# A graph attention network on one core: edges matched with sliding spans of 128 nodes, no running maximum, node work inside the edge loops

## The chip, the core and the metric

The kernel runs on one core of a Trainium2 chip. The engines are called here as the profile calls them: PE (TensorE; matmuls, and PEld its weight loads), DVE (VectorE), ACT (ScalarE), POOL (GpSimd, which also issues the indirect DMAs), SP (SyncE, which issues DMAs). The metric is the device time of one execution in microseconds (us), the median of several runs. A profile is one execution taken by the hardware profiler.

## What is computed

A graph has 6250 nodes and 100,000 edges (src, dst), sorted by dst, some 16 edges to a node, and an edge from each node to itself. Nodes have 768 numbers, all in float32. The reference, cut to what matters:

```python
def gat_conv(x, src, dst, W, a_src, a_dst, bias, heads):
    n = x.shape[0]
    h = (x @ W).reshape(n, heads, -1)
    alpha_s = (h * a_src[None]).sum(-1)
    alpha_d = (h * a_dst[None]).sum(-1)
    e = leaky_relu(alpha_s[src] + alpha_d[dst], 0.2)
    m = segment_max(e, dst, num_segments=n)
    e = exp(e - m[dst])
    denom = segment_sum(e, dst, num_segments=n)
    alpha = e / (denom[dst] + 1e-16)
    out = segment_sum(h[src] * alpha[:, :, None], dst, num_segments=n)
    return out.reshape(n, -1) + bias

# src, dst below: the edges and the loops
h = maximum(layernorm(x), 0)
h = relu(gat_conv(h, src, dst, W1, a_src1, a_dst1, b1, 4))   # 768 -> 4 heads of 64
h = relu(gat_conv(h, src, dst, W2, a_src2, a_dst2, b2, 1))   # 256 -> 1 head of 256
return x + relu(h @ Wm1 + bm1) @ Wm2 + bm2                   # 256 -> 256 -> 768
```

## The kernel before

Nodes lie in 49 tiles of 128 (the partitions). Edges lie in 98 chunks of 1024, each of 8 tiles of 128. Five stages follow one another:

1. **Nodes, first layer** (L187 to L211): for each node tile a layernorm, six transposes on PE (`tp`, L175) with evictions on DVE (`xT`, L176), six matmuls `h_ps` (L210); `keep_nodes` works out both scores with two products and a reduction on DVE (`pr`, `state`), puts features and source score as a row into a table in DRAM (`table<-row`) and the node's own edge into the accumulator `acc`.
2. **Edges, first layer** (`edges_in`, 98 chunks). `gather`: POOL issues 8 indirect DMAs, each of 128 rows of the table (`G`, L219); the source scores are transposed, stored to DRAM (`s_d`), and in `along` read back along the free dimension into all partitions (`S`, 512 KB per head) beside the chunk's destinations (`drow`, 512 KB). `greatest`: for the two node tiles that a chunk may reach, starting at a tile number loaded into a register, DVE makes the masks `mask` (nodes in the partitions), `pen` and `hot` (edges in the partitions), finds each node's greatest score (the fused add-and-maximum of L269, twice per head), and works out the new maximum `m` and the factor `fade` by which earlier sums shrink. `add`: matmuls `e_ps` with `mask` as the weights (L300, two for each edge tile) bring each edge its end's maximum and score, ACT takes the exponential, `hw` is the weighted rows, matmuls `o_ps` (L327, two for each edge tile) with `hot` as the weights sum them by node, and DVE scales and adds (`kept`, `acc`, L332 and L334).
3. **Nodes, second layer**: `aggregated` divides, adds the bias on POOL (`ob`, L398), applies relu and transposes; then matmuls `h_ps` (L412) and `keep_nodes`.
4. **Edges, second layer**: as 2, with one head; `hw` is made on ACT.
5. **Dense layers** (L428 to L449): `aggregated`, matmuls `m_ps` (L436) and `y_ps` (L445), residual, store.

A table can be gathered from only when all its rows are written, so each edge stage starts after all of the node stage ahead of it. All instructions of one engine run in one order; that order is not the one of the source but is fixed at build time by the framework's scheduler. Chunks that reach more than two node tiles would go through a loop behind each edge stage (L370); it turns zero times with these data. Matmuls of float32 operands appear in the profile as two records each.

Of the kernel before, what the change touches and what calls it, by code (L numbers as in the profile page):

```python
# [15 lines left out]
ENG = mybir.EngineType  # L16

P = 128
N = 6250          # nodes
E = 100000        # edges, self loops apart  # L20
# [6 lines left out]

NT = -(-N // P)   # node tiles
NTP = NT + 1      # and an empty one, so that two tiles can always be taken at once
TPC = 8           # edge tiles in a chunk  # L30
CH = P * TPC      # edges in a chunk
NCH = -(-E // CH)
PAD_DST = 1 << 20  # the destination of padding edges: no node
# [3 lines left out]
def kernel(  # L37
# [7 lines left out]
    a_src1: bass.AP,  # L45
    a_dst1: bass.AP,
    b1: bass.AP,
    W2: bass.AP,
    a_src2: bass.AP,
    a_dst2: bass.AP,  # L50
# [16 lines left out]
    dram_as = pool("dram_as", 4, space=bass.MemoryType.DRAM)  # L67
    sm = pool("sm", 3)
# [7 lines left out]
    ident = const.tile([P, P], F32, name="ident")  # L76
    make_identity(nc, ident)
    pidx = const.tile([P, 2], F32, name="pidx")
    nc.gpsimd.iota(pidx, pattern=[[P, 2]], base=0, channel_multiplier=1,
                   allow_small_or_imprecise_dtypes=True)  # L80
    iota2 = const.tile([P, 2 * P], F32, name="iota2")
    nc.gpsimd.iota(iota2, pattern=[[1, 2 * P]], base=0, channel_multiplier=0,
                   allow_small_or_imprecise_dtypes=True)
    first = const.tile([P, NTP], F32, name="first")
    nc.gpsimd.iota(first, pattern=[[P, NTP]], base=0, channel_multiplier=0,
                   allow_small_or_imprecise_dtypes=True)
    eps_c = const.tile([P, 1], F32, name="eps_c")
    nc.vector.memset(eps_c, EPS)

    att = {}  # L90
    for layer, s, d, b in ((1, a_src1, a_dst1, b1), (2, a_src2, a_dst2, b2)):
        for kind, v in (("s", s), ("d", d), ("b", b)):
            t = const.tile([P, HID], F32, name=f"att{layer}{kind}")
            nc.scalar.dma_start(t, bcast(v, HID))
            att[layer, kind] = t

# [1 line left out]
    src_i = const.tile([P, NCH * TPC], I32, name="src_i")  # L98
    nc.scalar.dma_start(src_i, src_cols)
    dst_f = const.tile([P, NCH * TPC], F32, name="dst_f")  # L100
    once = ctx.enter_context(ExitStack())
    ones = once.enter_context(tc.tile_pool(name="once", bufs=1))
    dst_i = ones.tile([P, NCH * TPC], I32, name="dst_i")
    nc.scalar.dma_start(dst_i, dst_cols)
    nc.vector.tensor_copy(dst_f, dst_i)

    dri = ones.tile([NCH, CH], I32, name="dri")
    nc.scalar.dma_start(dri, dst_rows)
    drf = ones.tile([NCH, CH], F32, name="drf")
    nc.vector.tensor_copy(drf, dri)  # L110
    dstf_d = dram.tile([NCH, CH], F32, name="dstf_d")
    nc.scalar.dma_start(dstf_d, drf)
    ends = const.tile([P, 2], F32, name="ends")
    nc.vector.tensor_reduce(ends[:NCH, 0:1], drf, AX.X, ALU.min)
    real = ones.tile([NCH, CH], F32, name="real")
    nc.vector.tensor_scalar(real, drf, float(N - 1), None, ALU.min)
    nc.vector.tensor_reduce(ends[:NCH, 1:2], real, AX.X, ALU.max)
    ends_i = const.tile([P, 2], I32, name="ends_i")
    nc.vector.tensor_copy(ends_i[:NCH], ends[:NCH])
    ends_t = const.tile([P, 2], I32, name="ends_t")  # L120
    nc.vector.tensor_scalar(ends_t[:NCH], ends_i[:NCH], 7, None, ALU.arith_shift_right)
    lohi_d = dram.tile([NCH, 2], I32, name="lohi_d")
    nc.scalar.dma_start(lohi_d, ends_t[:NCH])
    lohi = const.tile([1, NCH, 2], I32, name="lohi")
    nc.scalar.dma_start(lohi, bass.AP(tensor=lohi_d.tensor, offset=lohi_d.offset,
                                      ap=[[0, 1], [2, NCH], [1, 2]]))
    span = const.tile([1, NCH], F32, name="span")
    nc.vector.tensor_sub(span, lohi[:, :, 1], lohi[:, :, 0])
    wide = const.tile([1, 1], F32, name="wide")
    nc.vector.tensor_reduce(wide, span, AX.X, ALU.max)  # L130
    more = const.tile([1, 1], I32, name="more")
    nc.vector.tensor_scalar(more, wide, 2.0, float(NCH), ALU.is_ge, ALU.mult)
    once.close()

# [1 line left out]
    acc = const.tile([P, NTP, 4, HID // 4 + 1], F32, name="acc")  # L136
    nc.gpsimd.memset(acc[:, NT], 0.0)
    accf = acc.rearrange("p n h c -> p n (h c)")
    RW = 4 * (HID // 4 + 1)
    state = {}  # L140
    table = {}
    for layer, H in ((1, 4), (2, 1)):
        state[layer] = const.tile([P, NTP, 2, H], F32, name=f"state{layer}")
        nc.gpsimd.memset(state[layer][:, NT], 0.0)
        table[layer] = dram.tile([NT * P, HID + H], F32, name=f"table{layer}")

    def acc_view(H, sl):
        C = HID // H
        return accf[:, sl, :H * (C + 1)].rearrange("p n (h c) -> p n h c", h=H)

    def keep_nodes(wk, layer, H, i, h_ps):
        """A tile of nodes' features: into the table, and each node's own edge."""
        C = HID // H
        st = state[layer]
        row = wk.tile([P, HID + H], F32, name="row", tag="row")
        nc.scalar.activation(row[:, :HID], h_ps, AF.Copy)
        hv = h_ps.rearrange("p (h c) -> p h c", h=H)
        pr = wk.tile([P, 2, HID], F32, name="pr", tag="pr")
        nc.vector.tensor_mul(pr[:, 0], h_ps, att[layer, "s"])
        nc.vector.tensor_mul(pr[:, 1], h_ps, att[layer, "d"])  # L160
        nc.vector.tensor_reduce(st[:, i], pr.rearrange("p k (h c) -> p k h c", h=H), AX.X, ALU.add)
        nc.vector.tensor_copy(row[:, HID:], st[:, i, 0])
        av = acc_view(H, slice(i, i + 1))[:, 0]
        nc.scalar.activation(av[:, :, :C], hv, AF.Copy)
        nc.vector.memset(av[:, :, C:], 1.0)
        nc.sync.dma_start(table[layer][i * P:(i + 1) * P], row)

    def transposed(wk, t, k, name):
        """[128, k * 128] -> [128, k, 128], with each block transposed."""
        o = wk.tile([P, k, P], F32, name=name, tag=name)  # L170
        for k0 in range(0, k, 4):
            n = min(4, k - k0)
            p = ps.tile([P, 4, P], F32, name="tp", tag="tp")
            for j in range(n):
                nc.tensor.transpose(p[:, j], t[:, (k0 + j) * P:(k0 + j + 1) * P], ident)  # L175
            nc.vector.tensor_copy(o[:, k0:k0 + n], p[:, :n])  # L176
        return o
# [65 lines left out]
    def greatest(pools, layer, H, dcol, drow, S, b):  # L243
# [17 lines left out]
        for t in range(TPC):  # L261
            nc.vector.tensor_scalar(hot[:, t], iota2, drel[:, t:t + 1], None, ALU.is_equal)  # L262
# [218 lines left out]
```

## Time and profile before

| | |
|---|---|
| runs, us | 4979.31 median, 4977.9 to 4987.44 (3 runs) |
| span of the profiled execution | 5039.1 us, the only time that the profile gives for it |
| busy in it | PE 71%, DVE 65%, POOL 35%, ACT 15% of the span |
| first gather of layer 1, of layer 2 | 294.4 us, 3041.7 us |
| moved by DMA | 648 MB, 129 GB/s in the mean |

The profiled execution's span is 1.2% above the median of the runs. A row of a group reads: line, engine, operation, output<-inputs, shapes, count | busy us, mean ns of one | idle time of the engine just before them, and what ended it. A row of the timeline reads: start, duration (us), engine, line, operation, names, count and in brackets the idle time before it.

### The profile page before, as it was taken

The numbers are of one execution on the slowest core, as the hardware profiler recorded it, in microseconds if no ns is written. First come the engines' busy times: TensorE is split into PE (matmuls) and PEld (weight loads), VectorE is DVE, ScalarE is ACT, GpSimd is POOL, SyncE is SP. The second block draws the span as 40 slices with busy tenths as digits, with TensorE's granted clock in tenths as the row PEclk, the third lists the DMA queues.
The fourth block names the chain that finished last, engine by engine and source line by source line (L and its number), as shares of the span: only waits on it lengthen the run. The fifth ranks groups of instructions, "written<-read, shape, count | busy, mean of one in ns | idle before, by whom it ended". The sixth has DMA issues, their size and how long they took to land. (4 is left out here: it accounts for less than half of the span.)

```text
span 5039.1 us, 49714 instructions
## 1 busy us (share of the span) xinstructions
PE 3571.8 (71%) x14798; PEld 3086.7 (61%) x14799; DVE 3269.3 (65%) x9030; ACT 731.7 (15%) x2257; POOL 1783.9 (35%) x1728
## 2 busy tenths in 40 slices
PE   5636666666666666666666665888888888888888
PEld 4535555555555555555555544777777777777766
DVE  6757777777777777777777684555555555556544
ACT  3310000000000000000000031222222222222222
POOL 0033333333333333323333125344444444343345
PEclk9966666666666666666666676777777777777789
DMA  3344444444444444444444113333333333333345
GB/s 116 101 145 143 147 139 139 141 142 147 147 136 139 143 144 148 140 134 143 143 147 142 67 47 121 118 119 120 122 118 120 116 120 116 119 118 117 101 140 178
DMA packets 219275, 648.07 MB, mean 129 GB/s; under 512 B 42915, under 2 KB 61428, under 8 KB 218998
## 3 DMA queue, kind: packets, MB, share of 16 engines
q1 hardware_dynamic: 113060, 330.58, 19.3%
q0 software_dynamic: 75264, 207.63, 14.8%
q10 hardware_dynamic: 30674, 106.61, 5.9%
q8 instruction: 119, 1.95, 0.2%
q14 instruction: 158, 1.29, 0.1%
HBM read 610.07 MB, written 34.58 MB: 128 GB/s over the span
## 5 line engine op out<-in xcount | busy, mean ns | idle before, releaser
L219 POOL DMA_INDIRECT G<-table,src_i x1568 | 1624.3, 1036 | 2893.6 <-ACT hw L321 732.1
L327 PE MATMUL o_ps<-hw,hot 128*128 128x260 f32 (+1 forms) x6272 | 1755.7, 448 | 520.1 <-DVE hw L318 270.4
L327 PEld LDWEIGHTS o_ps<-hw,hot 128*128 128x128 f32 x6272 | 1419.0, 230 | 796.2 <-issue 522.0
L300 PE MATMUL e_ps<-m,mask 128*128 128x8 f32 (+1 forms) x6272 | 1323.7, 350 | 170.6 <-DVE m L281 170.6
L300 PEld LDWEIGHTS e_ps<-m,mask 128*128 128x128 f32 x6272 | 1321.4, 325 | 175.9 <-issue 136.2
L269 DVE CUSTOM_DVE_ANT_0 junk<-pen,S 128x1024 f32<-128x1024 bf16 x980 | 1193.5, 1218 | 38.1 <-DMA S<-s_d 19.6
L334 DVE TENSOR_TENSOR acc<-kept,o_ps 128x520 f32 (+1 forms) x196 | 135.8, 693 | 869.9 <-remote 592.7
L225 PE MATMUL s_ps<-ident,s_in 128*32 128x128 f32 (+1 forms) x196 | 63.7, 325 | 594.4 <-ACT s_in L224 512.1
L262 DVE TENSOR_SCALAR hot<-iota,drel 128x256 f32<-128x256 f32 x1568 | 448.3, 357 | 0.1
L303 DVE TENSOR_TENSOR z<-G,e_ps 128x32 f32<-128x32 f32 (+1 forms) x196 | 34.6, 177 | 623.0 <-PE e_ps L300 599.6
L225 PEld LDWEIGHTS s_ps<-ident,s_in 128*32 128x32 f32 (+1 forms) x196 | 17.8, 91 | 673.5 <-ACT s_in L224 582.4
L316 ACT ACTIVATE hw<-G,wt 128x256 f32<-128x256 f32 x784 | 323.7, 496 | 1.6
L224 ACT ACTIVATE s_in<-G 128x32 f32<-128x32 f32 (+1 forms) x196 | 46.4, 236 | 1820.9 <-DMA G<-table,src_i 1776.6
L258 DVE TENSOR_SCALAR mask<-drow,nid 128x1024 f32<-128x1024 f32 x392 | 298.3, 761 | 5.7 <-DMA drow<-dstf_d 5.7
L259 DVE TENSOR_SCALAR pen<-drow,nid 128x1024 bf16<-128x1024 f32 x392 | 293.6, 749 | 0.0
L318 DVE TENSOR_TENSOR hw<-G,wt 128x2048 f32<-128x2048 f32 x98 | 224.1, 2287 | 0.4 <-ACT wt L312 0.3
L210 PE MATMUL h_ps<-w,xT 128*128 128x256 f32 x588 | 146.3, 401 | 79.2 <-DVE xT L176 67.7
L312 ACT ACTIVATE wt<-dn 128x32 f32<-128x32 f32 (+1 forms) x196 | 42.9, 219 | 1006.3 <-DVE dn L310 846.5
L210 PEld LDWEIGHTS h_ps<-w,xT 128*128 128x128 f32 x588 | 113.1, 199 | 104.6 <-ACT xn L206 48.3
L288 ACT ACTIVATE fade<-fall 128x8 f32<-128x8 f32 (+1 forms) x196 | 39.6, 202 | 707.6 <-DVE fall L286 707.6
L445 PE MATMUL y_ps<-wm,mT 128*128 128x384 f32 x392 | 139.8, 500 | 3.1 <-ACT mT L440 1.2
L332 DVE TENSOR_TENSOR kept<-acc,fade 128x520 f32<-128x520 f32 (+1 forms) x196 | 135.4, 691 | 0.1
(81 smaller groups left out, 1949.3 us busy)
## 6 DMA issues: line engine op xcount, KB each, us to landing
S<-s_d SPq DMA_DIRECT2D x490, 512.0 KB
drow<-dstf_d ACTq DMA_DIRECT2D x196, 512.0 KB
xt<-in_x SPq DMA_DIRECT2D x96, 384.0 KB
G<-table,src_i POOLq DMA_INDIRECT x1568
out<-y SPq DMA_DIRECT2D x48, 384.0 KB
table<-row SPq DMA_DIRECT2D x49, 130.0 KB
table<-row SPq DMA_DIRECT2D x49, 128.5 KB
s_d<-s_sb SPq DMA_DIRECT2D x98, 16.0 KB
```

The lines of the kernel that those rows point to most:

```text
L210: nc.tensor.matmul(h_ps, xT[:, k], w1[:, k], start=(k == 0), stop=(k == KI - 1))
L219: nc.gpsimd.indirect_dma_start(out=G[:, t], out_offset=None, in_=table[layer], in_offset=bass.IndirectOffsetOnAxis(ap=idx[:, t:t + 1], axi ...
L258: nc.vector.tensor_scalar(mask[:, w], drow, nid[:, w:w + 1], None, ALU.is_equal)
L259: nc.vector.tensor_scalar(pen[:, w], drow, nid[:, w:w + 1], -BIG, ALU.not_equal, ALU.mult)
L262: nc.vector.tensor_scalar(hot[:, t], iota2, drel[:, t:t + 1], None, ALU.is_equal)
L269: nc.vector.tensor_tensor_reduce(out=junk, in0=pen[:, w], in1=S[h], scale=1.0, scalar=-BIG, op0=ALU.add, op1=ALU.max, accum_out=top[:, w, ...
L300: nc.tensor.matmul(e_ps[:, t], mask[:, w, t * P:(t + 1) * P], m[:, w, 1:3], start=(w == 0), stop=(w == 1))
L316: nc.scalar.activation(hw[:, t, 0, :C], G[:, t, :HID], AF.Copy, scale=wt[:, t])
L318: nc.vector.tensor_mul(hw[:, :, :, :C], G[:, :, :HID].rearrange("p t (h c) -> p t h c", h=H), wt.unsqueeze(3).to_broadcast([P, TPC, H, C]))
L327: nc.tensor.matmul(o_ps[:, w, :H * (C + 1)], hot[:, t, w * P:(w + 1) * P], hw[:, t].rearrange("p h c -> p (h c)"), start=(t == 0), stop=(t ...
L334: nc.vector.tensor_add(accf[:, ds(b, 2), :H * (C + 1)], kept[:, :, :H * (C + 1)], o_ps[:, :, :H * (C + 1)])
L445: nc.tensor.matmul(y_ps[:, s, :half], mT[:, j], wm2[:, j, s * half:(s + 1) * half], start=(j == 0), stop=(j == KH - 1))
```

## The change

The kernel is rewritten; the table gains a column of ones for each head.

- **Spans.** Edges are shifted by 256 empty ones and taken in 196 groups of 512 (4 tiles), one for each 32 nodes. Group g is matched with the 128 nodes from 32g - 64 on, so each edge tile has one span of nodes, not two tiles of them. Two groups (8 edge tiles) are a step u; there are 98 steps. Of 784 edge tiles 782 are worked on.
- **No maximum.** The weight of an edge, over a factor common to all edges of its end, is max(exp(s), exp(0.2 s) rho) with s the source's score and rho = exp(-0.8 d) of the end's score d. `prepare` makes rho for all nodes before a layer's edges, splits it into three bfloat16 parts and lays it out by spans (`win`). An edge gets rho by one bfloat16 matmul for each edge tile (`e_ps`, weights `mask`). `S`, `s_d`, `pen`, `top`, `fade`, `kept` and the register loads are gone.
- **Sums.** Each group's `o_ps` is added to the running span `acc`, of which the 32 nodes that left are cleared by `keep`; 32 finished nodes at a time are copied to `sum` by ACT.
- **Node work in the loops.** When a node tile is finished its own edge, division, transposes and matmuls (stages 3 and 5 above) run as `steps`, one step in each turn of the edge loop. Scores come out of the node matmuls as extra columns (`with_scores`). Nothing but gathers is left on POOL in the edge loops.
- **General path.** At the end four flags (a score above 20 in either layer, an edge below or above its span) decide whether the old algorithm runs over everything (`general`).

Its core, new lines alone (`G` has 5 buffers, `rows` 2, `hot` 3, `mask` and `hw` 2, each tag in PSUM 2):

```diff
+        s, d = sd[layer][:, :, :H], sd[layer][:, :, H:]
+        rho = wk.tile([P, NT, H], F32, name="rho")
+        nc.scalar.activation(rho, d, AF.Exp, scale=SLOPE - 1.0)
...
+        e1 = wk.tile([P, NT, H], F32, name="e1")
+        nc.scalar.activation(e1, s, AF.Exp)
+        e2 = wk.tile([P, NT, H], F32, name="e2")
+        nc.scalar.activation(e2, s, AF.Exp, scale=SLOPE)
+        v = wk.tile([P, NT, H], F32, name="v")
+        nc.vector.tensor_mul(v, e2, rho)
+        own = wk.tile([P, NT, H], F32, name="own")
+        nc.vector.tensor_max(own, v, e1)
...
+            def gather(u):
+                G = gp.tile([P, 8, TW[layer]], F32, name="G")
+                for t in tiles(u):
+                    k = 8 * u + t
+                    nc.gpsimd.indirect_dma_start(
+                        out=G[:, t], out_offset=None, in_=table[layer],
+                        in_offset=bass.IndirectOffsetOnAxis(ap=src_i[:, k:k + 1], axis=0))
+                return G
...
+            def match(u):
+                if u % 2 == 0:
+                    drow[0] = rows.tile([P, 2, 8 * P], BF16, name="drow")
+                    n = min(2, NU - u)
+                    nc.sync.dma_start(
+                        drow[0][:, :n].rearrange("p u e -> p (u e)"),
+                        bcast(dmod_d, n * 8 * P, u * 8 * P))
+                T = tiles(u)
...
+                mask = eg.tile([P, 8 * P], BF16, name="mask")
+                nc.vector.tensor_tensor(mask[:, t0 * P:(t0 + n) * P],
+                                        drow[0][:, u % 2, t0 * P:(t0 + n) * P],
+                                        pidx_b.to_broadcast([P, n * P]), ALU.is_equal)
+                hot = eg.tile([P, 8, P], F32, name="hot", bufs=3)
+                nc.vector.tensor_tensor(
+                    hot[:, t0:t0 + n], iota.unsqueeze(1).to_broadcast([P, n, P]),
+                    dcol[:, 8 * u + t0:8 * u + t0 + n].unsqueeze(2).to_broadcast([P, n, P]),
+                    ALU.is_equal)
+                e_ps = ps.tile([P, 8, 3 * H], F32, name="e_ps", tag="tp")
+                for t in T:
+                    g = 2 * u + t // TPG
+                    nc.tensor.matmul(e_ps[:, t], mask[:, t * P:(t + 1) * P], win[:, g + 1],
+                                     start=True, stop=True)
+                return hot, e_ps
...
+                sc = G[:, T, RW[1]:] if layer == 1 else G[:, T, HID:HID + 1]
+                e1 = sm.tile([P, 8, H], F32, name="e1")
+                nc.scalar.activation(e1[:, T], sc, AF.Exp)
+                e2 = sm.tile([P, 8, H], F32, name="e2")
+                nc.scalar.activation(e2[:, T], sc, AF.Exp, scale=SLOPE)
+                rho = sm.tile([P, 8, H], F32, name="rho")
+                nc.vector.tensor_reduce(rho[:, T], e_ps[:, T].rearrange("p t (h k) -> p t h k", k=3),
+                                        AX.X, ALU.add)
+                v = sm.tile([P, 8, H], F32, name="v")
+                nc.vector.tensor_mul(v[:, T], e2[:, T], rho[:, T])
+                w = sm.tile([P, 8, H], F32, name="w")
+                nc.vector.tensor_max(w[:, T], v[:, T], e1[:, T])
+                if layer == 2:
+                    hw = eg.tile([P, 8, P], F32, name="hw")
+                    nc.vector.tensor_mul(hw[:, T], hot[:, T],
+                                         w[:, T].to_broadcast([P, n, P]))
+                else:
+                    hw = eg.tile([P, 8, H, C + 1], F32, name="hw")
+                    nc.vector.tensor_mul(
+                        hw[:, T], G[:, T, :RW[1]].rearrange("p t (h c) -> p t h c", h=H),
+                        w[:, T].unsqueeze(3).to_broadcast([P, n, H, C + 1]))
+                return hw
...
+                    T = [t for t in tiles(u) if t // TPG == half]
+                    o_ps = ps.tile([P, RW[layer]], F32, name="o_ps", tag="o")
+                    for t in T:
+                        if layer == 2:
+                            l, r = hw[:, t], G[:, t]
+                        else:
+                            l, r = hot[:, t], hw[:, t].rearrange("p h c -> p (h c)")
+                        nc.tensor.matmul(o_ps, l, r, start=(t == T[0]), stop=(t == T[-1]))
...
+                        nc.vector.tensor_copy(acc, o[half])
+                    else:
+                        nc.vector.scalar_tensor_tensor(acc, run[0], keep[:, (g + 1) % 4:(g + 1) % 4 + 1],
+                                                       o[half], ALU.mult, ALU.add)
...
+                        nc.scalar.activation(done[t][r], acc[r], AF.Copy)
...
+            for i in range(NU + 3):
+                a, b, c, d = i, i - 1, i - 2, i - 3
+                if a < NU:
+                    G[a] = gather(a)
+                if 0 <= d < NU:
+                    o = spread(d, G.pop(d), H_.pop(d)[0], W_.pop(d))
+                if 0 <= b < NU:
+                    H_[b] = match(b)
+                if 0 <= c < NU:
+                    W_[c] = weigh(c, G[c], *H_[c])
+                if 0 <= d < NU:
+                    gather_up(d, o)
+                advance()
...
+        def mean1(t, sum_, own):
+            C = HID // 4
+            mine = wk.tile([P, 4, C + 1], F32, name="mine")
+            nc.vector.tensor_mul(mine, heads_row(rows1.pop(t)),
+                                 own[:, t].unsqueeze(2).to_broadcast([P, 4, C + 1]))
+            all_ = wk.tile([P, 4, C + 1], F32, name="all_")
+            nc.vector.tensor_add(all_, mine, sum_.rearrange("p (h c) -> p h c", h=4))
+            rden = wk.tile([P, 4], F32, name="rden")
+            nc.vector.reciprocal(rden, all_[:, :, C])
+            o = wk.tile([P, HID], F32, name="o")
+            nc.vector.tensor_mul(o.rearrange("p (h c) -> p h c", h=4), all_[:, :, :C],
+                                 rden.unsqueeze(2).to_broadcast([P, 4, C]))
+            return o
...
+        layer_edges(1, 4, [mean1, lambda t, o, own: turned(wk, 1, o), features2], fetch1)
...
+        layer_edges(2, 1, [mean2, lambda t, o, own: turned(wk, 2, o), dense1, dense2], fetch2)
...
+    is_bad = nc.values_load(bad_i, min_val=0, max_val=1)
+    with tc.If(is_bad):
+        general(ctx, tc, locals())
```

**How the order of instructions changes.** First place: the edge loop of layer 1, in its steady course. On PE stood, chunk by chunk (s_ps is the transpose of the scores):

```order
L225 MATMUL s_ps<-ident,s_in 32x128
L300 MATMUL e_ps<-m,mask 128x8 x16
L327 MATMUL o_ps<-hw,hot 128x260 x16
L225 MATMUL s_ps<-ident,s_in 32x128
L300 MATMUL e_ps<-m,mask 128x8 x32
```

Now the same engine has, the pair of its first two rows eight times in each step:

```order
L305 LDWEIGHTS mask
L305 MATMUL e_ps<-win,mask 128x12
L348 MATMUL o_ps<-hw,hot 128x260 x8
L408 MATMUL tp<-ident,o 128x128 x2
L441 MATMUL h_ps<-w_2073,rT 128x258
```

For 8 edge tiles there are 8 matmuls with `hot` where there were 16, and 8 with `mask` where there were 16; a transpose pair and two `h_ps` stand in every second step. On DVE, same place, one of the two parts of a chunk was:

```order
L251 TENSOR_SCALAR nid<-pidx,base 128x2
L281 SCALAR_TENSOR_TENSOR m<-both 128x2x8
L318 TENSOR_TENSOR hw<-G,wt 128x32x64
L286 TENSOR_TENSOR fall<-m 128x8
L253 TENSOR_SCALAR drel<-dst_f,base 128x8
L258 TENSOR_SCALAR mask<-drow,nid 128x1024
L259 TENSOR_SCALAR pen<-drow,nid 128x1024
L258 TENSOR_SCALAR mask<-drow,nid 128x1024
L259 TENSOR_SCALAR pen<-drow,nid 128x1024
L269 ISA junk,top<-pen,S 128x1024
L269 ISA top 128x1
```

Now DVE has, over some more than one step (`acc` twice in a step, once for each half):

```order
L363 SCALAR_TENSOR_TENSOR acc<-acc,keep,o_ps 128x260
L298 TENSOR_TENSOR hot<-iota,dcol 128x1024
L430 TENSOR_TENSOR all__2602<-mine,sum 128x260
L320 TENSOR_REDUCE rho<-e_ps 128x32
L432 RECIPROCAL rden<-all__2602 128x4
L363 SCALAR_TENSOR_TENSOR acc<-acc,keep,o_ps 128x260
L434 TENSOR_TENSOR o<-all__2602,rden 128x256
L323 TENSOR_TENSOR v<-e_2642,rho 128x32
L294 TENSOR_TENSOR mask<-drow,pidx_b 128x1024
L325 TENSOR_TENSOR w<-v,e_2640 128x32
L363 SCALAR_TENSOR_TENSOR acc<-acc,keep,o_ps 128x260
L332 TENSOR_TENSOR hw<-G,w 128x2080
```

The eight rows of L269 for a chunk are gone, `mask` and `hot` are one instruction each, and `all_`, `rden` and `o` of the node work stand between them; here the second `acc` of a step stands ahead of the next step's `hw`.

Second place: the edge loop of layer 2 on PE. Before:

```order
L225 MATMUL s_ps<-ident,s_in 8x128
L300 MATMUL e_ps<-m,mask 128x2 x32
L327 MATMUL o_ps<-hw,hot 128x257 x16
L225 MATMUL s_ps<-ident,s_in 8x128
L327 MATMUL o_ps<-hw,hot 128x257 x16
```

Now, over two steps (with `m_ps` x4 between the next `e_ps`):

```order
L305 MATMUL e_ps<-win,mask 128x3
L498 MATMUL y_ps<-wm_8366,mT 128x384
L348 MATMUL o_ps<-G,hw 128x258 x8
L498 MATMUL y_ps<-wm_8366,mT 128x384 x3
L408 MATMUL tp<-ident,o 128x128 x2
L348 MATMUL o_ps<-G,hw 128x258 x8
```

The dense layers' matmuls, a stage of their own before, have moved between the edge matmuls.

More of the change, by code (lines that the diff above doesn't have):

```diff
@@ L131 @@
[L131 to L177, printed above, removed]
+    ones_c = const.tile([P, 1], F32, name="ones_c")
+    nc.vector.memset(ones_c, 1.0)
@@ new lines @@
+    TW = {1: RW[1] + 4, 2: RW[2]}
+    table, sd = {}, {}
+    for layer, H in heads.items():
+        table[layer] = dram.tile([NT * P, TW[layer]], F32, name=f"table{layer}")
+        sd[layer] = const.tile([P, NT, 2 * H], F32, name=f"sd{layer}")
+    bT = {}
+    for layer, b in ((1, b1), (2, b2)):
+        bT[layer] = const.tile([P, KH], F32, name=f"bT{layer}")
+        with nc.allow_non_contiguous_dma(reason="256 numbers"):
+            nc.scalar.dma_start(bT[layer], b.rearrange("(k p) -> p k", p=P))
@@ L206 @@
             nc.scalar.activation(xn, xt, AF.Relu, bias=shift, scale=rstd)
-            xT = transposed(wk, xn, KI, "xT")
-            h_ps = ps.tile([P, HID], F32, name="h_ps", tag="mm")
+            xT = wk.tile([P, KI, P], F32, name="xT")
+            for k0 in range(0, KI, 4):
+                n = min(4, KI - k0)
+                p = ps.tile([P, 4, P], F32, name="tp", tag="tp")
+                for j in range(n):
+                    nc.tensor.transpose(p[:, j], xn[:, (k0 + j) * P:(k0 + j + 1) * P], ident)
+                nc.vector.tensor_copy(xT[:, k0:k0 + n], p[:, :n])
@@ L209 @@
+            h_ps = ps.tile([P, HID + 8], F32, name="h_ps", tag="mm")
             for k in range(KI):
                 nc.tensor.matmul(h_ps, xT[:, k], w1[:, k], start=(k == 0), stop=(k == KI - 1))
[L211 to L230 removed]
```

717 lines of the change are left out of this document (466 added, 251 removed).

## The prediction

> **What bounds the kernel now.** I read the page's busy times first, then busy times by stage, the waits, the groups and short stretches of the timeline.
>
> ```profile
> span 5039.1 us, 49714 instructions
> PE 3571.8 (71%) x14798; PEld 3086.7 (61%) x14799; DVE 3269.3 (65%) x9030; ACT 731.7 (15%) x2257; POOL 1783.9 (35%) x1728
> ```
>
> No engine fills the span. By stage (columns: stretch, its length, busy us and count of PE, PEld, DVE, ACT, POOL, then granted PE clock, DMA share, GB/s):
>
> ```profile
> 0.00:294.40 294.40, 179.28 (x882) 148.74 (x883) 201.93 (x626) 98.63 (x198) 1.59 (x13) 0.97 0.31 99
> 294.40:2806.00 2511.60, 1561.38 (x6136) 1364.29 (x6136) 1821.51 (x4368) 118.42 (x480) 868.30 (x784) 0.66 0.44 144
> 2806.00:3041.70 235.70, 153.26 (x530) 112.10 (x529) 175.27 (x571) 55.31 (x158) 35.68 (x49) 0.70 0.13 43
> 3041.70:4835.00 1793.30, 1487.59 (x6383) 1331.17 (x6384) 975.34 (x3252) 414.84 (x1278) 759.77 (x789) 0.72 0.38 117
> 4835.00:5040.00 205.00, 190.27 (x871) 130.42 (x869) 95.28 (x214) 44.53 (x143) 118.51 (x93) 0.97 0.54 183
> ```
>
> Rows 2 and 4 are the edge stages, 85% of the span: 25.6 us a chunk in layer 1 (DVE 73% busy, PE 62%), 18.3 in layer 2 (PE 83%). POOL works a third to two fifths of both and stands the rest:
>
> ```profile
> ACT s_in L224 <- DMA G<-table,src_i: 1776.6, 192, 16.9
> ACT wt L312 <- DVE dn L310: 846.5, 102, 19.0
> POOL G L219 <- ACT hw L321: 732.1, 47, 17.2
> DVE z L303 <- PE e_ps L300: 599.6, 194, 7.7
> ```
>
> So gathers wait for a buffer that the arithmetic frees, and the arithmetic waits in turns between DVE and PE. This is what the change cuts, and the question is what comes next.
>
> **POOL's price.** The change leaves 782 gathers for each layer (784 before). First all gathers, then those of the first 41 us of layer 1, then what DVE did in those 41 us:
>
> ```profile
> L219 POOL DMA_INDIRECT G<-table,src_i x1568 | 1624.3, 1036 | 2893.6 <-ACT hw L321 732.1 <-DVE drel L253 544.5 <-DVE fall L286 525.6
> L219 POOL DMA_INDIRECT G<-table,src_i x32 | 31.5, 983 | 301.7 <-DMA table<-row 292.2 <-issue 9.4
> L269 DVE CUSTOM_DVE_ANT_0 junk<-pen,S 128x1024 f32<-128x1024 bf16 x9 | 11.0, 1225 | 22.2 <-issue 14.9 <-DMA S<-s_d 7.1
> L258 DVE TENSOR_SCALAR mask<-drow,nid 128x1024 f32<-128x1024 f32 x4 | 3.2, 804 | 5.7 <-DMA drow<-dstf_d 5.7
> ```
>
> 32 gathers without a wait for anything took 31.5 us and 9.4 of "issue" between them: (31.5 + 9.4) / 32 = 1.28 us each. The quickest and a slow one:
>
> ```profile
> 1009.22 0.74 DVE L258 TENSOR_SCALAR mask<-drow,nid 128x1024 f32<-128x1024 f32 x1
> 1009.36 1.42 POOL L219 DMA_INDIRECT G<-table,src_i  x1 [17.75 <-DVE fall L286]
> ...
> 1020.27 0.95 POOL L219 DMA_INDIRECT G<-table,src_i  x1 [0.30 <-issue]
> 1024.31 0.26 ACT L224 ACTIVATE s_in<-G 128x32 f32<-128x32 f32 x1 [14.90 <-DMA G<-table,src_i]
> ```
>
> The floor is 0.95 + 0.30 = 1.25 us with DVE still; beside `mask` (one input, 1024 in 0.74 us) a gather took 1.42; with the mean of all it is 1.036 + 0.30 = 1.34. A gather has landed 3.1 us after its end (1021.22 to 1024.31). Step u needs 8 gathers: 10.0, 10.2 or 10.7 us. I take 1.28, since the changed loop has no instruction like `mask` of L258 left, but many with two inputs like L269, which filled 11 of those 41 us. Ends: 1.25 and 1.34.
>
> The Trainium skill's page "SBUF — State Buffer", section "Who interferes with whom", speaks against this: a DVE instruction with two SBUF inputs shuts out a GpSimd instruction that reads SBUF, for its whole length, and nearly all of DVE's work here now is such. By the same section one-input instructions in the two-port mode do it too; the row of 1.42 agrees with that. If each gather lost the time of such instructions, the sum would be that of rival 2. The 32 gathers lost 32 x (0.983 - 0.95) = 1.1 us beside 11.0 us of L269, so the trace bears the full lock out for a tenth at most.
>
> **DVE and PE beside it.** Prices:
>
> ```profile
> L318 DVE TENSOR_TENSOR hw<-G,wt 128x2048 f32<-128x2048 f32 x98 | 224.1, 2287 | 0.4 <-ACT wt L312 0.3
> L334 DVE TENSOR_TENSOR acc<-kept,o_ps 128x520 f32 x98 | 68.2, 696 | 272.9 <-PE o_ps L327 212.0 <-remote 47.6 <-issue 13.3
> L160 DVE TENSOR_TENSOR pr<-h_ps,att1d 128x256 f32<-128x256 f32 x49 | 20.3, 413 | 0.0
> L303 DVE TENSOR_TENSOR z<-G,e_ps 128x32 f32<-128x32 f32 x98 | 18.4, 187 | 419.2 <-PE e_ps L300 419.2
> L448 DVE TENSOR_TENSOR y<-xb,y_ps 128x768 f32<-128x768 f32 x49 | 46.6, 953 | 47.6 <-PE y_ps L445 40.0 <-DMA out<-y 5.0 <-POOL ob L398 2.0
> L164 ACT ACTIVATE acc<-h_ps 128x256 f32<-128x256 f32 x98 | 36.5, 372 | 18.7 <-DVE pr L160 18.5
> L224 ACT ACTIVATE s_in<-G 128x32 f32<-128x32 f32 x98 | 25.3, 258 | 1244.6 <-DMA G<-table,src_i 1207.4 <-DVE hot L262 26.3 <-DVE top L269 10.8
> ```
>
> DVE, layer 1, a step: `mask` and `hot` 2 x 1.22 (as L269, 1024 elements; as L258 it would be 0.80), `rho` 0.25, `v` and `w` 0.37, `hw` 2.32 (2080 elements), `acc` 2 x 0.42, node work (three of 256 at 0.41, a reciprocal as L303, each second step) 0.7: 6.9 us. Layer 2: 3 x 1.22, 0.55, 0.84, and half of the node work (residual 0.95 as L448, `all_` 0.42, reciprocal 0.17, two `y` 1.1) 1.3: 6.4. ACT, layer 1: two exponentials 0.52 (as L224), two copies 0.74 (as L164), half of a tile's `rT`, row and scores (1.3) 0.65: 1.9. All under 10.2.
>
> PE depends on the clock. At the full clock 32 records took 7.12 us, at a mixed one 10.16; e_ps' 32 records of before follow:
>
> ```profile
> 3107.81 7.12 PE L327 MATMUL o_ps<-hw,hot 128*128 128x257 f32 x32
> 2759.44 10.16 PE L327 MATMUL o_ps<-hw,hot 128*128 128x260 f32 x32 [7.87 <-DVE hw L318]
> 1007.01 6.96 PE L300 MATMUL e_ps<-m,mask 128*128 128x8 f32 x32 [4.14 <-DVE m L281]
> ```
>
> A step has 16 records of `o_ps`: 3.6 us. The new `e_ps` (8 matmuls, bfloat16) isn't in the trace: between 0 and 8 x 2 x 0.22 = 3.5 us; I take 0.9, a quarter, as float32 has two records, each longer. Node work per step: layer 1 half of (4 records of `tp` and 4 of `h_ps`) 0.7, layer 2 half of (`tp`, 8 of `m_ps` at 0.11, 8 of `y_ps` at 0.36) 2.1. Sum 5.1 and 6.5 us at full clock, 10.2 and 13.0 at half. At the 0.66 and 0.72 granted before: 7.8 and 9.1. Both hide under POOL's 10.2, in layer 2 barely; I add 20 us there for steps in which they don't.
>
> The waits that the order adds: the first `acc` stands behind `v` on DVE, which waits for `G` to land; `hw` behind the other half's `acc`, which waits for PE. From landing: exponentials 0.5, `v`, `acc`, `w`, `mask` 2.0, `hw` 2.3, `o_ps` 3.6 to 7.1, `acc` 0.4: 8.8 to 12.3, of which the next step overlaps all but PE's part and `hw`, so no step needs over 10.2. The buffer of `G` is free some 13 to 25 us after its gathers end; with five, POOL comes back to it after 4 x 10.2 us. On SP's queue `drow` (512 KB for two steps, where each chunk had six such loads in layer 1 and two in layer 2) stands behind stores of rows, which wait for ACT; with two buffers it has 20 us to spare.
>
> **Stage 1.**
>
> ```profile
> 109.74 0.82 PE L175 MATMUL tp<-ident,xn 128*128 128x128 f32 x6
> 111.08 0.68 DVE L176 COPY xT<-tp 128x512 f32<-128x512 f32 x1
> 111.90 2.83 PE L210 MATMUL h_ps<-w,xT 128*128 128x256 f32 x12 [1.35 <-DVE xT L176]
> 114.57 0.82 PE L175 MATMUL tp<-ident,xn 128*128 128x128 f32 x6
> ```
>
> A tile takes 4.83 us; `xT` came late behind `pr` and `state` (0.41 + 0.41 + 0.67), which are gone. Then `h_ps` can start 0.55 + 0.1 + 0.68 after `tp`: 1.35 + 2.92 (264 columns) = 4.3; 49 tiles 211 us. The start grows by the load of W1's transpose and the score matmuls, some 3 us on 31. The last part, from the last `h_ps` to the first gather, was 5 us and stays. First gather at 250 us, not 294.4.
>
> **The sum.** 250 + 782 x 1.28 = 1001 for layer 1. Then layer 2 needs the last table rows: landing 3.1, exponentials and `v`, `w` 0.9, `hw` 2.3, `o_ps` 5.3 (between the clocks), `acc` 0.4, three copies 1.1, mean 1.0, `tp` and `rT` 1.3, `h_ps` and row 1.7, store 3.0, hand-offs 2: 22 us. This replaces the stage of 235.7 us. Layer 2: 1001 + 20. Its end: landing 3.1, exponentials to `w` 0.9, `hw` 1.2, `o_ps` 5.3, `acc` 0.4, copies 1.1, mean 1.0, `tp` and `rT` 1.3: 14; `m_ps`, `mT`, `y_ps`, `y` and store 11; the check on DVE (five passes over 784 columns, 4.5 us) with flag and branch 8: 33; it replaces the stage of 205. Total 250 + 1001 + 22 + 1021 + 33 = 2327 us of span. The runs' median is 0.988 of the span shown: 2300 us.
>
> **Rivals.**
> 1. *PE paces.* For: layer 2's 6.5 us at full clock, and bursts broken up by waits were at 0.66. Against: the clock rose where PE was busy (0.97 in rows 1 and 5). It takes over below a mean clock of 6.5 / 10.2 = 0.64; at 0.55 layer 2 gets 98 x (11.8 - 10.2) = 157 us longer, at 0.5 274: 2450, up to 2600 with layer 1 touched.
> 2. *DVE shuts POOL out* while an instruction with two SBUF inputs runs. In full, each step gets longer by 5.3 us in layer 1 (`mask`, `hot` 2.44, `hw` 2.32, `v`, `w` 0.37, half of `mine` 0.2) and 4.5 in layer 2 (three of 1.22, `v`, `w` 0.3, half of 1.0): 98 x 9.8 = 960 of span, 3250 us. Half of it: 2770. Against: the 32 gathers.
> 3. *The general path runs* (the other side). It would follow the whole fast path. Its chunks don't overlap: each pays the gathers 10, the landing 3 and DVE's time of a chunk in turn (1821.51 / 98 = 18.6 us in layer 1, 975.34 / 98 = 10.0 in layer 2, with PE's left out): 98 x (31.6 + 23.0) = 5350 on top of 2327, so 7700 us at least. It decides when a single edge lies outside its span or a score is over 20. Worked out from the inputs, edges lie 44 to 97 nodes into their spans of 128 and layer 1's scores stay under 3. Nearly excluded.
>
> **Chances.** POOL paces at 1.25 to 1.34 us a gather: 0.63, 2200 (floor, short ends) to 2420. Rival 1: 0.18, 2400 to 2600. Rival 2 in part or full: 0.15, 2450 to 3250. General path: 0.01; something unseen the rest. The range 2180 to 2600 leaves out most of rival 2. 0.2% is about what a measurement can tell from no change: faster 0.98, same 0.005, slower 0.015.
>
> **What the new profile would show.** POOL above 80% busy with "issue" as the main end of its idle time in both edge stages; gathers of 0.95 to 1.04 us; DVE and PE at two thirds; stage 1 near 250 us; under 25 us between the layers' gathers. I am wrong if POOL waits for `G`'s readers (PE or DVE paces), or if gathers last over 1.1 us.

## The result, and the profile after

The changed kernel takes 2575.22 us (median of 4 runs, 2569.64 to 2578.76) against 4979.84 us: ratio 0.5168, 95% interval 0.5159 to 0.5176. The forecast was 2300 us, its range 2180 to 2600: the direction and the pace-maker were right, the time was 275 us longer. First the busy times, then the stretches as before: up to the first gather, layer 1's gathers, between the layers, layer 2's gathers, the end.

```profile
span 2567.9 us, 22404 instructions
PE 1429.3 (56%) x6784; PEld 1114.5 (43%) x6785; DVE 1324.1 (52%) x2458; ACT 448.5 (17%) x1434; POOL 1761.1 (69%) x1672
```

```profile
0.00:254.00 254.00, 184.80 (x906) 151.35 (x907) 134.96 (x372) 88.04 (x199) 16.85 (x108) 0.99 0.39 122
254.00:1418.60 1164.60, 537.36 (x2546) 416.20 (x2546) 602.11 (x1001) 159.78 (x565) 926.65 (x782) 0.71 0.45 123
1418.60:1454.00 35.40, 23.46 (x102) 17.79 (x102) 22.82 (x49) 10.23 (x33) 0.00 (x0) 0.79 0.24 75
1454.00:2509.70 1055.70, 650.54 (x3073) 503.78 (x3074) 538.73 (x984) 179.24 (x607) 817.63 (x782) 0.78 0.56 162
2509.70:2567.90 58.20, 33.15 (x159) 25.35 (x157) 25.44 (x54) 11.19 (x32) 0.00 (x0) 0.83 0.14 49
```

Both edge stages have lost more than 40%, the two node stages most of theirs. In rows 2 and 4 POOL is busy 80% and 77%, DVE 52% and 51%, PE 46% and 62%. The groups of the gather and of DVE's long instructions, and the waits:

```profile
L276 POOL DMA_INDIRECT G<-table,src_i x1564 | 1744.3, 1115 | 514.8 <-issue 455.8
L298 DVE TENSOR_TENSOR hot<-iota,dcol 128x1024 f32<-128x1024 f32 (+1 forms) x196 | 238.0, 1214 | 0.0
L332 DVE TENSOR_TENSOR hw<-G,w 128x2080 f32<-128x2080 f32 (+1 forms) x98 | 226.8, 2314 | 0.7 <-DMA G<-table,src_i 0.3
```

```profile
ACT e L318 <- DMA G<-table,src_i: 781.2, 88, 11.8
DVE acc L363 <- PE o_ps L348: 508.0, 127, 11.3
POOL G L276 <- issue: 455.8, 1496, 0.4
```

POOL's idle time between gathers is 0.30 us each and ends by "issue": it waits for no reader of `G`, and the exponentials wait for gathers. POOL paces. But a gather takes 1115 ns in the mean, not the 980 (1.28 us less the gap of 0.30) of the forecast, and more than the 1.1 us that the prediction had named as a sign of being wrong. The timeline of layer 1 shows which ones are long:

```profile
705.01 0.95 POOL L276 DMA_INDIRECT G<-table,src_i  x1 [0.30 <-issue]
706.26 0.95 POOL L276 DMA_INDIRECT G<-table,src_i  x1 [0.30 <-issue]
706.28 0.48 DVE L363 SCALAR_TENSOR_TENSOR acc<-acc,keep,o_ps 128x260 f32<-128x260 f32 x1 [8.56 <-PE o_ps L348]
706.68 2.33 DVE L332 TENSOR_TENSOR hw<-G,w 128x2080 f32<-128x2080 f32 x1
707.51 2.32 POOL L276 DMA_INDIRECT G<-table,src_i  x1 [0.30 <-issue]
...
709.32 1.22 DVE L298 TENSOR_TENSOR hot<-iota,dcol 128x1024 f32<-128x1024 f32 x1
710.13 1.23 POOL L276 DMA_INDIRECT G<-table,src_i  x1 [0.30 <-issue]
711.66 0.95 POOL L276 DMA_INDIRECT G<-table,src_i  x1 [0.30 <-issue]
```

`hw` ends at 709.01. The gather that started in it ends 0.82 us after that; the one that started in `hot` (end 710.54) again 0.82 after. The gather of 706.26 had begun before `hw` and took its 0.95. Sorted by what DVE was doing when a gather started, the trace gives:

| DVE at the start of a gather | layer 1: gathers, us lost over 0.946 each | layer 2 |
|---|---|---|
| `hw` (two operands in SBUF) | 97, 135.9 | 18, 11.3 |
| `mask` (two) | 94, 35.0 | 59, 35.4 |
| `hot` (two) | 49, 13.7 | 91, 27.2 |
| `acc` (one in SBUF, one in PSUM) | 42, 0.0 | 92, 0.0 |
| nothing | 428, 0.0 | 381, 0.0 |

All losses: 187 and 78 us. The theory to test: a gather that starts while DVE runs an instruction with both operands in SBUF stands until that instruction is through; this is called the lock below. Rivals: PE or DVE paces the loops after all; any DVE work, or the DMA traffic, lengthens gathers.

### The profile page after: what moved, and what is told of

Read it like the earlier page. It is cut to its first block, busy times and chain, and to the rows that moved or that the text cites. A ratio compares the mean times of both kernels' runs of the same rounds, so it can differ in the third digit from the quotient of the medians.

```text
span 2567.9 us, 22404 instructions
## 1 busy us (share of the span) xinstructions
PE 1429.3 (56%) x6784; PEld 1114.5 (43%) x6785; DVE 1324.1 (52%) x2458; ACT 448.5 (17%) x1434; POOL 1761.1 (69%) x1672
## 5 line engine op out<-in xcount | busy, mean ns | idle before, releaser
L276 POOL DMA_INDIRECT G<-table,src_i x1564 | 1744.3, 1115 | 514.8 <-issue 455.8
L348 PE MATMUL o_ps<-G,hw 128*128 128x258 f32 x1564 | 438.0, 442 | 21.1 <-DVE hw L328 12.8
L363 DVE SCALAR_TENSOR_TENSOR acc<-acc,keep,o_ps 128x260 f32<-128x260 f32 (+1 forms) x390 | 185.6, 476 | 508.3 <-PE o_ps L348 508.0
L348 PE MATMUL o_ps<-hw,hot 128*128 128x260 f32 x1564 | 417.2, 426 | 54.5 <-DVE hw L332 52.3
L348 PEld LDWEIGHTS o_ps<-G,hw 128*128 128x128 f32 x1564 | 354.6, 230 | 109.1 <-issue 23.0
L348 PEld LDWEIGHTS o_ps<-hw,hot 128*128 128x128 f32 x1564 | 337.6, 219 | 123.8 <-DVE hw L332 57.7
L298 DVE TENSOR_TENSOR hot<-iota,dcol 128x1024 f32<-128x1024 f32 (+1 forms) x196 | 238.0, 1214 | 0.0
L294 DVE TENSOR_TENSOR mask<-drow,pidx_b 128x1024 bf16<-128x1024 bf16 (+1 forms) x196 | 237.3, 1212 | 0.1
L332 DVE TENSOR_TENSOR hw<-G,w 128x2080 f32<-128x2080 f32 (+1 forms) x98 | 226.8, 2314 | 0.7 <-DMA G<-table,src_i 0.3
L374 ACT ACTIVATE sum<-acc 32x260 f32<-32x260 f32 (+1 forms) x392 | 163.2, 416 | 228.4 <-DVE acc L363 220.9
L206 PE MATMUL h_ps<-w,xT 128*128 128x264 f32 x588 | 146.6, 400 | 37.3 <-DVE xT L203 37.3
```

Source lines behind the costliest of these rows:

```text
L206: nc.tensor.matmul(h_ps, xT[:, k], w1[:, k], start=(k == 0), stop=(k == KI - 1))
L276: nc.gpsimd.indirect_dma_start(out=G[:, t], out_offset=None, in_=table[layer], in_offset=bass.IndirectOffsetOnAxis(ap=src_i[:, k:k + 1], a ...
L294: nc.vector.tensor_tensor(mask[:, t0 * P:(t0 + n) * P], drow[0][:, u % 2, t0 * P:(t0 + n) * P], pidx_b.to_broadcast([P, n * P]), ALU.is_equal)
L298: nc.vector.tensor_tensor(hot[:, t0:t0 + n], iota.unsqueeze(1).to_broadcast([P, n, P]), dcol[:, 8 * u + t0:8 * u + t0 + n].unsqueeze(2).to ...
L332: nc.vector.tensor_mul(hw[:, T], G[:, T, :RW[1]].rearrange("p t (h c) -> p t h c", h=H), w[:, T].unsqueeze(3).to_broadcast([P, n, H, C + 1]))
L348: nc.tensor.matmul(o_ps, l, r, start=(t == T[0]), stop=(t == T[-1]))
```

## Experiments

Each time stands beside runs of the kernel before on the same chip. Line numbers differ a little between the kernels.

**1. Operands moved to PSUM (four kernels, one job on one chip).** `iota`, `pidx` and `w` are put into a bank of PSUM (`aux`; for the bank `y_ps` has one buffer), all three, or `w` alone:

```
-  hot[...], iota.unsqueeze(1)...          +  hot[...], aux[:, :P].unsqueeze(1)...
-  mask[...], drow..., pidx_b...           +  mask[...], drow..., aux[:, P:P + 1]...
-  w = sm.tile([P, 8, H], F32)             +  w = aux[:, o0:o0 + 8 * H]      # o0 by u % 3
```

> `iota`, `pidx` and `w` are read from PSUM, so that `mask`, `hot` and `hw` have one operand in SBUF instead of two; lengths and count of all instructions as in the changed kernel. Theory (a gather that starts while a DVE instruction with two SBUF operands runs stands until that instruction ends): the 187 + 78 us that the gathers of the two layers lost over 0.946 us each vanish, gathers of 0.95 us throughout, 1.25 us from one to the next, 2575 - 265 = 2310 us (2295 to 2340). Rival A (PE or DVE paces the loops): no change, 2575. Rival B (any DVE work, or the DMA traffic, lengthens gathers): no change, 2575, gathers still 1.12 us in the mean.

> Only `w` is read from PSUM: `hw` alone has one operand in SBUF. Theory: gathers that started in `hw` lost 136 us in layer 1 and 11 in layer 2; these vanish, and what starts in `mask` and `hot` stays or grows a little: 2575 - 147 = 2428 us (2400 to 2470). Rivals A and B: 2575.

The other two add an unused instruction like `hot`, with `iota` from SBUF or from `aux`.

> One more instruction like `hot` in each edge step (1024 elements, both operands in SBUF, result unused). Theory: the 196 instructions cost as `mask` and `hot` do now, 0.14 to 0.37 us each, mean 0.28: 55 us more, 2630 us (2600 to 2680); DVE busy 240 us more. Rival A with DVE as the pace: 196 x 1.22 = 239 us more, 2815; with PE: 2575.

> The same added instruction, but with its first operand in PSUM. Theory: DVE is busy 240 us more and the time doesn't change, 2575 us (2555 to 2595). Rival A with DVE: 2815. Rival B (any DVE work lengthens gathers): as the run with both operands in SBUF, about 2630.

Measured: 2772, 2741, 2691 and 2714 us, the kernel before 5041 on this chip. All times missed. The gathers did what the theory says: with all three in PSUM the 163 that started in layer 1's `hw` or `hot` lost under 0.5 us together. With `w` alone there, `hw` cost nothing, and `mask` and `hot`, still in SBUF, 49 us in layer 1 and 104 in layer 2. In layer 2 of the other two, 85 gathers that started in the added instruction lost 87.3 us with its operand in SBUF, and 86 lost 0.2 us with it in PSUM. (In layer 1 the added one reads only constants, and the scheduler had put it ahead of the loop.) Yet the first kernel was the slowest. Its timeline:

```profile
950.84 0.35 PE L309 MATMUL e_ps<-win,mask 128*128 128x12 bf16 x8
951.02 0.20 PEld L413 LDWEIGHTS tp<-ident,o 128*128 128x128 f32 x2
951.04 0.42 PE L413 MATMUL tp<-ident,o 128*128 128x128 f32 x2
...
960.61 0.94 POOL L280 DMA_INDIRECT G<-table,src_i  x1 [0.30 <-issue]
964.26 0.26 DVE L324 TENSOR_REDUCE rho<-e_ps 128x32 f32<-128x96 f32 x1 [12.92 <-remote]
964.31 0.37 ACT L416 ACTIVATE rT<-tp,bT 128x128 f32<-128x128 f32 x1 [9.60 <-remote]
...
967.73 0.94 POOL L280 DMA_INDIRECT G<-table,src_i  x1 [6.18 <-ACT sd L451]
```

("remote": the profile knows no giver of the signal.) `rho` and `rT` wait for PE alone, whose matmuls had ended at 951.5, and both start 12.8 us later; then POOL waits for `G`. An instruction that waits for PE alone and starts over 1 us after PE's last record (a late signal, below) occurs some 160, 70, 16 and 75 times in these four traces, and not once in the changed kernel's. Did the edits or the chip do it?

**2. The control, the bank unused, and the node work taken out (another job, another chip).** The last moves the node steps behind the loop (`sum` gets 49 buffers for it):

```
-                advance()
-            while ready:
-                advance()
+            late, ready[:] = list(ready), []
+            while late or ready:
+                if late:
+                    prefetch(late[0][0])
+                    ready.append(late.pop(0))
+                advance()
```

> The changed kernel again, as the control of the four runs with operands in PSUM, which came out at 2691 to 2772 us against a kernel before of 5041 there. Theory C (the chip of those runs delays PE's signals: in their traces instructions that waited for PE alone started up to 13 us after PE's last record, 17 to 161 times a run, in the changed kernel's first trace never): such late signals here too, and 2620 to 2700 us. Theory O (the edits, since each makes the scheduler order the instructions anew): no late signals, 0.517 of the kernel before, 2575 to 2610 us.

> One bank of PSUM set aside (`y_ps` with one buffer) and filled, but not read in the loops: `hot`, `mask` and `hw` as in the changed kernel, the order of layer 1's loop too. Theory O: layer 1 as the control; layer 2, whose order differs, up to 100 us longer with late signals there. Theory C: late signals in the control as well, and the two within 1%. If neither, the single buffer of `y_ps` shows as DVE or PE waiting for it in layer 2 alone.

> The node work (mean, transposes, second features, MLP) is taken out of the edge loops and done behind each of them, as the kernel before did: 49 tiles of 3 to 4.5 us behind layer 1 and 4.5 to 5 behind layer 2, a part of that overlapped. Theory: the edge stages stay paced by POOL and give back little (7 us of gathers that started in node work's DVE instructions), the two stages cost 150 to 220 us each: 2575 + 350 = 2925 us (2850 to 3020). Rival (the node work inside paces the loops): the edge stages fall by as much as is added, 2575 to 2650.

Measured: control 2586 us (ratio 0.5193); bank unused 2657; node work behind 2846; before 4979. None of the three traces has a late signal, though the second has the same bank and `y_ps` in one buffer. That kernel's layer 1 is the control's (1179 us of gathers, 1182), and its layer 2 has 69 us more (1124 against 1056): 28 gaps of POOL with 41 us above the usual 0.30 each, and 28 us of longer gathers. So setting the bank aside costs layer 2 some 69 us in this order of instructions (in experiment 3 the same setting leaves 5 us of such gaps), and it doesn't bring the late signals. The control ran on another chip than the four, so that it can't tell by itself whether that chip or the edits brought them; experiment 3 does.

The stretches with the node work behind:

```profile
254.80:1414.80 1160.00, 602.21 (x2322) 471.86 (x2322) 556.88 (x780) 111.13 (x384) 922.07 (x782) 0.71 0.40 113
1414.80:1528.00 113.20, 76.11 (x340) 57.11 (x340) 73.71 (x273) 56.93 (x215) 0.06 (x2) 0.92 0.51 129
1528.00:2590.70 1062.70, 608.13 (x2300) 451.91 (x2300) 436.95 (x770) 111.43 (x379) 824.79 (x782) 0.73 0.43 123
2590.70:2845.90 255.20, 208.75 (x916) 138.51 (x916) 128.81 (x264) 80.58 (x258) 0.00 (x0) 0.93 0.56 171
```

The gathers take 1160 and 1063 us (control 1182 and 1056): inside the loops the node work costs at most 22 us, outside 78 and 197 us more than in the control. That part of the change is worth 260 us, against 350 expected, just under the range. The other 2130 are the rest of the change, nearly all of it in the edge stages (2512 and 1793 us before, 1160 and 1063 here).

**3. The lock without late signals (third job).** The first kernel of all again; then the same in layer 1 alone, with both buffers of `y_ps`; then `hw` of layer 1 in eight pieces with all operands in SBUF:

```
-  nc.vector.tensor_mul(hw[:, T], G[:, T, :RW[1]]..., w[:, T]...)
+  for t in range(t0, t0 + n):
+      nc.vector.tensor_mul(hw[:, t], G[:, t, :RW[1]]..., w[:, t]...)
```

> The kernel with all three operands in PSUM again, in a job of its own, since its first runs shared a chip on which PE's signals came late (the control, on another chip, had none). Theory (lock): without late signals the gathers' 0.94 us tells in the time: layer 1's gathers take 985 to 1010 us instead of 1182, layer 2's 1010 to 1050 (the single buffer of `y_ps` cost it some 40), and the time is 2586 - 190 - 25 = 2370 us (2320 to 2430). Rival (the new order of instructions, not the chip, made POOL wait for `G`): POOL stands in gaps over 0.32 us again, 460 us of them, and it takes over 2550 us on any chip.

> As that, but in layer 1 alone, and `y_ps` keeps its two buffers (the bank is lent to layer 1 only); layer 2 as in the changed kernel. Theory: layer 1's gathers in 985 to 1010 us, layer 2's in 1056 as in the control: 2586 - 185 = 2400 us (2370 to 2430). Rival (order): layer 1 no shorter, 2550 to 2600.

> Layer 1's `hw` as eight instructions of 260 elements, all with two operands in SBUF: some 0.42 us each as those of 260 in the node work, 3.4 us a step instead of 2.3. Theory (a gather that starts in one waits for that one's end alone): no gather loses over 0.3 us to `hw`; of its 136 to 147 us some 25 are left, layer 1's gathers 1065 us, 2586 - 115 = 2470 us (2440 to 2530), with 105 us more of DVE. Rival (all of DVE's two-operand time is lost to gathers, or DVE's length counts): as long as the control or longer, 2586 to 2690.

Measured: 2365 us (0.4756, 0.4745 to 0.4768), 2413 (0.4848, 0.4840 to 0.4856) and 2592 (0.5211, 0.5201 to 0.5220); before 4976. The first two came out as the theory had it (2370, 2400), and none of the three traces has a late signal. The first one's timeline and group, to be held against the changed kernel's:

```profile
699.31 2.31 DVE L337 TENSOR_TENSOR hw<-G,aux 128x2080 f32<-128x2080 f32 x1
699.90 0.95 POOL L280 DMA_INDIRECT G<-table,src_i  x1 [0.30 <-issue]
701.16 0.94 POOL L280 DMA_INDIRECT G<-table,src_i  x1 [0.30 <-issue]
```

```profile
L280 POOL DMA_INDIRECT G<-table,src_i x1564 | 1508.2, 964 | 521.1 <-issue 463.1
L337 DVE TENSOR_TENSOR hw<-G,aux 128x2080 f32<-128x2080 f32 (+1 forms) x98 | 225.9, 2305 | 0.6 <-DMA G<-table,src_i 0.2
```

`hw` is as long as ever (2305 ns, 2314 in SBUF), and two gathers start in it and take 0.95. Layer 1's gathers fell from 1182 us to 986 and layer 2's from 1056 to 1003, with DVE and PE doing the same work: neither paced. DMA moved 145 GB/s in layer 1's gathers, 121 in the control's, so that its traffic hadn't lengthened them either. Of these 249 us some 25 were lost again, 15 of them in stage 1, whose instructions stand in another order. The control ran on another chip; but the split kernel, whose layer 2 is the control's, ran on this one, with 1054 us of gathers there.

The split missed. Its pieces were 0.42 us each and DVE's time for `hw` 273 us, but gathers that started in them still lost 149 us:

```profile
703.91 2.79 DVE L333 TENSOR_TENSOR hw<-G,w 128x260 f32<-128x260 f32 x8
704.62 4.04 POOL L276 DMA_INDIRECT G<-table,src_i  x1 [0.30 <-issue]
706.63 1.21 DVE L298 TENSOR_TENSOR hot<-iota,dcol 128x1024 f32<-128x1024 f32 x1
707.76 0.24 DVE L320 TENSOR_REDUCE rho<-e_ps 128x32 f32<-128x96 f32 x1
```

That gather ends 0.82 us after `hot`: it stood through six pieces and `hot`, until `rho`, which reads PSUM, came. 43 of 141 lost about 3.1 us like this, and nearly all others 0.1 to 0.3, what was left of their own piece. The trace tells them apart by the moment of their start: of 49 gathers that start in the first 30 ns of a piece, when the piece before hasn't quite ended, 44 stood through pieces behind it, and of the 92 that start later in a piece none did. Why the first 30 ns count isn't shown. So a gather can stand through a chain of such instructions, not only through the one in which it starts.

**4. One put back, and one more taken out (fourth job, both on the kernel with all three in PSUM).** The first adds `mask` once more as it was, with both operands in SBUF and its result unused; the second adds layer 2's last bias by PE:

```
-            nc.vector.tensor_add(xt, xt, bm2b)
+                nc.tensor.matmul(y_ps, ones_r, bm2b[:, s * half:(s + 1) * half],
+                                 start=False, stop=True)
```

> The kernel with all three operands in PSUM (2365 us), and one instruction with two SBUF operands put back into each step: `mask` as it was, 1024 elements, its result unused. Theory (lock): such a `mask` cost layer 1's gathers 35 to 41 us and layer 2's 35 to 37 in the changed kernel, 0.38 us each; 196 of them make it 2365 + 75 = 2440 us (2400 to 2490), with gathers that start in that instruction 0.4 to 0.6 us longer and all others at 0.94. Rival (what fell with the operands in PSUM was something else, such as the order of instructions): 2365 us, or up to 2400 from 237 us more of DVE.

> As the kernel with all three operands in PSUM, and the bias `bm2b` of layer 2 is added by a matmul with a row of ones into `y_ps`, not by DVE to `xt`: the last long instruction with two SBUF operands of layer 2 is gone. Theory (lock): 40 gathers lost 20 us in it; 2365 - 20 = 2345 us (2330 to 2360), layer 2's gathers 985 us. Rival (in layer 2 PE is near its limit and pays 49 x 2 x 2 records more): 2365 to 2400.

Measured: 2392 us (0.4803, 0.4795 to 0.4810) and 2334.5 (0.4685, 0.4678 to 0.4693); before 4980. Put back, it cost 27 us, a third of what was expected. By the time alone the rival (up to 2400) can't be told from the theory (2400 to 2490); the gathers decide. 148 started in the added instruction and lost 62 us (0.42 each, as expected), while those in `mask`, `hot` and `hw` beside it still lost nothing. But in layer 2 the loss in the bias add fell from 20 us to 1.5 at the same time, and layer 2 got no longer (1002 us). What one instruction costs depends on how POOL's and DVE's courses fall against each other. Without the bias add the gathers are at the floor:

```profile
L280 POOL DMA_INDIRECT G<-table,src_i x1564 | 1487.2, 951 | 513.5 <-issue 457.9
```

Layer 2's take 978 us, 1.250 each. This kernel is the fastest: 0.4685 against 0.5193 of the control, 10% less.

## Why the prediction was right and wrong

- **POOL paces both loops**: right. Shown by the waits, and by experiment 3, where shorter gathers gave 221 us against the control. Rival 1 (PE) is out: PE's clock was 0.71 and 0.78 in the loops, above its 0.64. PE's work was priced high, 7.8 and 9.1 us a step where it took 5.5 and 6.6.
- **1.28 us a gather**: the step that failed. It was 1.489 us in layer 1 (1164.6 / 782) and 1.350 in layer 2, 164 and 55 us more; of this, 20 in layer 2 had been set aside for PE, which needed none. This was rival 2 in part, which had a chance of 0.15. That 2575 us lies in the stated range is luck: its upper end, 2600, was set for rival 1, which didn't occur, and POOL at 1.25 to 1.34 us a gather had been given 2200 to 2420. The price came from 32 gathers beside nine instructions of 1.22 us, read as "a tenth at most". Against the 5.3 and 4.5 us of two-input work in a step (519 and 441 us a layer) the gathers lost 187 and 78, that is 36% and 18%. The trace of before had the full lock in that very row (L269 and the gathers alone, from its timeline):

```profile
318.06 1.23 DVE L269 CUSTOM_DVE_ANT_0 junk<-pen,S 128x1024 f32<-128x1024 bf16 x1 [14.89 <-issue]
318.63 1.47 POOL L219 DMA_INDIRECT G<-table,src_i  x1 [0.30 <-issue]
...
325.71 1.23 DVE L269 CUSTOM_DVE_ANT_0 junk<-pen,S 128x1024 f32<-128x1024 bf16 x1
326.79 0.96 POOL L219 DMA_INDIRECT G<-table,src_i  x1 [0.30 <-issue]
326.98 1.23 DVE L269 CUSTOM_DVE_ANT_0 junk<-pen,S 128x1024 f32<-128x1024 bf16 x1
328.06 0.97 POOL L219 DMA_INDIRECT G<-table,src_i  x1 [0.30 <-issue]
```

  Each of these gathers ends 0.82 us after the instruction in which it started, as in the changed kernel. Eight of the 32 started in such an instruction. Two had 0.65 and 0.25 us of it before them and lost 0.53 and 0.11; the other six had 0.15 and lost 0.02 at most. For here DVE repeats every 1.27 us, hardly slower than POOL: a gather that was held starts its successor 0.82 + 0.30 = 1.12 us after the instruction's end, which is 0.15 before the end of the next one. The two had fallen into step where the lock costs nearly nothing. In the changed kernel `hw`, 2.31 us long, comes once in a step of eight gathers, and the 97 that started in it in layer 1 lost 1.4 us each. Over the whole trace of before, 479 gathers started in L269 and lost 98 us.
- **The rule that was weighed and set aside** was the better guide. The section "Who interferes with whom" of the Trainium skill's page "SBUF — State Buffer" says that a DVE instruction with two SBUF inputs contends with a GpSimd instruction that reads SBUF, and one with at most one, outside the two-port modes, doesn't: the runs agree (0.95 us in `hw` with `w` in PSUM, 2.32 with both in SBUF). It gives no time for a gather; here a gather loses if it starts in such an instruction, and then, chains aside, the rest of it less about 0.13 us. One SBUF input alone is no safeguard: `mask` of the kernel before has one, and the gather of 1.42 us that the prediction shows beside it also ended 0.82 us after it (1009.96 to 1010.78).
- **Stage 1**, 250 us: 254.0, right.
- **Between the layers**, 22 us: 35.4. The term `o_ps` 5.3 was for one step, but steps before it were still in PE's queue (its `o_ps` rows):

```profile
1424.01 4.45 PE L348 MATMUL o_ps<-hw,hot 128*128 128x260 f32 x16
1429.52 3.77 PE L348 MATMUL o_ps<-hw,hot 128*128 128x260 f32 x16 [0.88 <-DVE hw L332]
1435.48 7.28 PE L348 MATMUL o_ps<-hw,hot 128*128 128x260 f32 x32 [0.32 <-DVE hw L332]
```

  That is 15.5 us in place of 5.3.
- **The end**, 33 us: 58.2. The last `y` came 39 us after the last gather, not 25, since the `y` of three tiles still stood behind the last `o_ps` (2530.9); the check took 5 as reckoned, and flag and branch 14 where 3.5 were left for them.
- **Span to median**: the factor 0.988; here it is 2575.2 / 2567.9 = 1.003, some 38 us. It was no factor to carry over: each run on record takes some 2 us more than its own span. The profile of before shows an execution of 5039 us, where the runs beside it took 4979; 5041 is what that kernel takes on the chip of experiment 1.

Together: 2327 + 4 + 164 + 13 + 35 + 25 = 2568 us of span. The general path didn't run.

## What to carry to other kernels

Where GpSimd issues gathers back to back, look at what DVE runs when a gather starts: in these kernels a `tensor_tensor` with both operands in SBUF stopped that gather, and with one of them in PSUM it cost nothing and took no longer itself. Price such a contention from single events, how long after the other's end the held one ends, and not from the mean of a stretch: two engines that have fallen into step hide it. And a drain at the end of a loop costs every step that is in flight, not the last one.

## What the runs showed of the hardware that was not expected

- Two-input DVE instructions that follow each other can hold a gather through all of them (4.04 us), as 44 of the 49 did that started in the first 30 ns of a piece; cutting one into pieces gained nothing.
- The same kernel took 2772 us on one chip and 2365 on another, the kernel before 5041 and 4976. On the first, instructions that waited for PE alone started up to 21 us late; of the traces of the other experiments none has a single one. (The trace of the kernel before, with that chip's 5039 us, has 29, at most 2 us late.) Whether it was that chip or that hour, and why the kernels with freer gathers suffered more (some 160 and 70 times, against 16), stays open. One lead: in the first kernel's trace 70 of them fall 2.6 to 3.0 us after the end of the last gather ahead of a pause of POOL, as the 964.26 of experiment 1 does behind 961.55; in the second kernel's they don't cluster there.
